# An order written out for the last unit of a quantized feed-forward, with accumulator banks in rotation, on one Trainium2 core

## The chip, the cores and the metric

One core of a Trainium2 chip. The metric is the device time of one execution in microseconds, the median of several runs. The engines named below are TensorE (PE in the profile; PEld is its weight load), VectorE (DVE), ScalarE (ACT), GpSimd (POOL) and SyncE (SP), which only starts transfers. Each engine has its own queue and works through it in order; an instruction that waits holds all that stands behind it on its engine.

## The reference

Two layers, each a conditioner (a linear map with a low-rank adapter chosen per batch) followed by a gated feed-forward, with a residual. The change lies in the second layer, whose feed-forward has weights of 4-bit integers with one scale for each 128 inputs:

```python
# x: (8, 128, 512), conditioner of layer 1
base_out = einsum('bti,oi->bto', x, W) + b
lora_out = einsum('btr,bro->bto', einsum('bti,bir->btr', x, A), Bm)
h = base_out + lora_out * 2.0
# feed-forward of layer 1: H = 512, I = 1792, groups of G = 128
W = q.reshape(O, In // G, G) * s[:, :, None]        # for gate, up and down
d = silu(einsum('bsh,ih->bsi', h, Wg)) * einsum('bsh,ih->bsi', h, Wu)
x = x + einsum('bsi,hi->bsh', d, Wd)
```

## The kernel before

All activations lie with features on partitions: `x[o]`, o = 0 to 3, holds 128 features of all 1024 tokens, and a "half" (tb = 0 or 1) is 512 tokens, the columns that one accumulator bank (PSUM) holds in float32. There are 8 banks.

**The conditioner of layer 1** makes h, four tiles of 128 features, as the sum of two parts, `hi` (rounded to the type float32r, in which these matmuls run) and `lo` (what the rounding left). Its products are made by a scheme with few multiplications, so results come out as sums of banks and helper tiles. The loop at lines 1300 to 1310 ends it: for m = 0 and 1, `l_added` (VectorE, line 1272) adds a bank to u[m], `l_finish` writes hi on ACT (line 1264) and then lo on VectorE (line 1266) for tile m, half 1; the same is then done with v[m] for tile m + 2, half 0. So h 3, half 0, is what comes last.

**The feed-forward** runs in 14 units f of 128 of the 1792 inner features. A unit has 8 products for gate (s = 0) and up (s = 1), one for each scale group k = 0 to 3, and, two units later (`LAG`), 4 products for down, one for each o. The integers are used as weights directly; the scale is applied when a bank is read. One product over 512 tokens is two matmuls, hi and lo (`summed`, line 1328). How each product leaves its banks:

- `scaled` without an addend runs on ACT (line 1334): it writes a fresh sum, or a copy `y` of a down product.
- `scaled` with an addend runs on VectorE (line 1337): bank times scale plus what is there, into `sum` or straight into `x[o]`.
- `added` runs on GpSimd (line 1343), for four things: the two partial gate sums are added (`gate_added`), the up sum is multiplied by the silu (`gated_q`), the lo part of the activation is made (`rest`, tile `act_lo`), and a copy y is added to x (`y_added`).
- ACT also makes the silu (line 1395) and the hi part of the activation (`first_bits`, line 1404, tile `act_hi`).

Thus a unit goes: gate sums, `gate_added` (GpSimd), silu (ACT), up sums, `gated_q` (GpSimd), `first_bits` (ACT), `rest` (GpSimd), and after that its down products may run. GpSimd also issues the loads of the integer weights (lines 1220 and 1222); the loads of units 10 to 13 wait until an earlier unit's buffer is free, and so are issued among the additions.

Units 0 to 12 run in the loop at line 1413, which sets the order on every engine. There a product covers both halves (two banks, a "pair", 4 matmuls, 1024 columns), with four pairs in rotation. The last unit, f = 13, and the down products of units 11, 12 and 13 run after it, by halves, in single banks taken from a pool of eight: first all eight products of half 0 with the down products of unit 11 between them, then half 1, then down of unit 12, then down of unit 13, each half of x[o] being stored when it has its last addend. Six halves of down products go through ACT, y and GpSimd there (o = 1 of units 11 and 12, half 0 of o = 3 of unit 12, half 0 of o = 1 of unit 13); the others are added by VectorE. The stores are at line 1515, on SP and ACT.

Of the kernel before, what the change touches and what calls it, by code (L numbers as in the profile page):

```python
# [7 lines left out]
F32 = mybir.dt.float32  # L8
# [3 lines left out]
ALU = mybir.AluOpType  # L12

P = 128
NB = 8
T = 1024
TB = 512
NTB = T // TB
# [16 lines left out]
WARM = 2  # L35
NS = H + NF * P
LAG = 2


@with_exitstack  # L40
def kernel(
# [1219 lines left out]
    def l_finish(o: int, tb: int, of):  # L1261
        hi, lo = (part[o][:, halves[tb]] for part in parts)
        plus = lb[:, o : o + 1]
        in_order(nc.scalar.activation(hi, of, AF.Identity, bias=plus))
        in_order(
            nc.vector.scalar_tensor_tensor(  # L1266
                lo, of, plus, hi.bitcast(F32), op0=ALU.add, op1=ALU.subtract
            )
        )

    def l_added(to, ps, plus):
        in_order(nc.vector.tensor_tensor(to, ps, plus, ALU.add))
# [27 lines left out]
    for m in two:  # L1300
        l_sum(3, m, "22", 5, False)
        l_sum(4, m, "T4", None, False)
        expand(
            [[None, banks[5, m]], [banks[4, m], None]], b1, [m * P, (m + 2) * P], [tl, tl],
            go_on={(0, 1)},
        )
        l_added(u[m], banks[5, m], u[m])
        l_finish(m, 1, u[m])
        l_added(v[m], banks[4, m], v[m])
        l_finish(m + 2, 0, v[m])  # L1310


# [6 lines left out]
    def pair(name: str):  # L1319
        return pairs.tile([P, NTB, TB], F32, tag="pair", name=name)  # L1320
# [4 lines left out]
    def summed(ps, w, src, at):  # L1325
        for n, part in enumerate(src):
            in_order(
                nc.tensor.matmul(ps, w, part[:, at], start=(n == 0), stop=(n == len(src) - 1))  # L1328
            )

    def scaled(to, ps, scale, plus=None):

        if plus is None:
            in_order(nc.scalar.activation(to, ps, AF.Identity, scale=scale))  # L1334
        else:
            in_order(
                nc.vector.scalar_tensor_tensor(  # L1337
                    to, ps, scale, plus, op0=ALU.mult, op1=ALU.add
                )
            )  # L1340

    def added(to, a, b, op):
        in_order(nc.gpsimd.tensor_tensor(to, a, b, op))  # L1343

    def unit_tile(what: str, f: int, bufs: int, dtype=F32):
        return l1.tile([P, T], dtype, tag=what, name=f"{what}_{f}", bufs=bufs)

    def gate_or_up(f: int, s: int, k: int, at=whole, into=None):


        on_act = k == 0 or (s == 0 and k == 2)
        if on_act and (f, s, k) not in sums:
            sums[f, s, k] = unit_tile(f"sum{s}{k}", f, 2)
        to = sums[f, s, k - k % 2 if s == 0 else 0][:, at]
        w, src = ready["q", f][0][:, s, k, :], [part[k] for part in parts]
        if into is None:
            both = pair(f"gu{s}_q{f}_{k}")
            for tb in range(NTB):
                summed(both[:, tb], w, src, halves[tb])
            ps = both.rearrange("p b s -> p (b s)")  # L1360
        else:
            summed(into, w, src, at)
            ps = into
        scaled(to, ps, sg[:, f, s, k : k + 1], None if on_act else to)

    def gate_added(f: int, at=whole):
        added(sums[f, 0, 0][:, at], sums[f, 0, 0][:, at], sums[f, 0, 2][:, at], ALU.add)

    def down_group(f: int, o: int, on_act=False, at=whole, into=None):
        w, src, scale = ready["q", f][1][:, bass.ts(o, P)], acts["q", f], sd[:, o, f : f + 1]  # L1370
        if into is None:
            both = pair(f"d_q{f}_{o}")
            for tb in range(NTB):
                summed(both[:, tb], w, src, halves[tb])
            ps = both.rearrange("p b s -> p (b s)")
        else:
            summed(into, w, src, at)
            ps = into
        to = x[o][:, at]
        if on_act:  # L1380
            if (f, o) not in ys:
                ys[f, o] = unit_tile("y", f"{f}_{o}", 2)
            scaled(ys[f, o][:, at], ps, scale)
        else:
            scaled(to, ps, scale, to)

    ys = {}

    def y_added(f: int, o: int, at=whole):
        added(x[o][:, at], x[o][:, at], ys[f, o][:, at], ALU.add)  # L1390

    def silu(f: int, at=whole):
        if ("sil", f) not in sums:
# [3 lines left out]
    def gated_q(f: int, at=whole):  # L1397
        if ("q", f) not in acts:
            acts["q", f] = [unit_tile(f"act_{w}", f, 3, F32R) for w in ("hi", "lo")]
        up = sums[f, 1, 0][:, at]  # L1400
        added(up, up, sums["sil", f][:, at], ALU.mult)

    def first_bits(f: int, at=whole):
        in_order(nc.scalar.copy(acts["q", f][0][:, at], sums[f, 1, 0][:, at]))  # L1404

    def rest(f: int, at=whole):
        hi, lo = acts["q", f]
        added(lo[:, at], sums[f, 1, 0][:, at], hi[:, at].bitcast(F32), ALU.subtract)
# [4 lines left out]
    for f in range(NF - 1):  # L1413
        d = f - LAG
        if d > 0 and d - 1 + QBUFS < NF:
            load_q(d - 1 + QBUFS)
        gate_or_up(f, 0, 0)
        if 0 < f <= LAG:
            silu(f - 1)
        gate_or_up(f, 0, 1 if f else 2)  # L1420
        if f:
            gated_q(f - 1)
        if d >= 0:
            down_group(d, 0)
        gate_or_up(f, 0, 2 if f else 1)
        if f:
            first_bits(f - 1)
            rest(f - 1)
        gate_or_up(f, 0, 3)
        gate_added(f)  # L1430
        if d >= 0:
            down_group(d, 1)
        for k in range(3):
            gate_or_up(f, 1, k)
        if d >= 0:
            down_group(d, 3, True)
            y_added(d, 3)
        if f >= LAG:
            silu(f)
        gate_or_up(f, 1, 3)  # L1440
        if d >= 0:
            down_group(d, 2)
# [2 lines left out]

    in_pairs.close()
    last = ctx.enter_context(
        tc.tile_pool(name="last", bufs=8, space=bass.MemoryType.PSUM, reuse_waits="tile")
    )

    def single(name: str):
        return last.tile([P, TB], F32, tag="bank", name=name)

    def down_half(f: int, o: int, tb: int, on_act: bool):
        down_group(f, o, on_act, halves[tb], single(f"d_q{f}_{o}_{tb}"))

    def down_halves(f: int, o: int, on_act: bool):
        for tb in range(NTB):
            down_half(f, o, tb, on_act)

    def y_halves_added(f: int, o: int):
        for at in halves:
            y_added(f, o, at)

    f = NF - 1

    def half_unit(s: int, k: int, tb: int):
        gate_or_up(f, s, k, halves[tb], single(f"gu{s}_q{f}_{tb}_{k}"))

    at = halves[0]  # L1470
    for s in range(2):
        for k in range(KC):
            half_unit(s, k, 0)
            if (s, k) == (0, 1):
                gated_q(f - 1)
            if (s, k) == (0, 2):
                first_bits(f - 1)
                rest(f - 1)
            if (s, k) == (0, 3):
                gate_added(f, at)  # L1480
            if k % 2 == 1:
                o = 2 * s + k // 2
                down_halves(f - LAG, o, o == 1)
                if o == 1:
                    y_halves_added(f - LAG, o)
            if (s, k) == (1, 0):
                silu(f, at)
    gated_q(f, at)

    d, at = f - 1, halves[1]
    for k in range(KC):
        half_unit(0, k, 1)
    gate_added(f, at)
    half_unit(1, 0, 1)
    silu(f, at)
    half_unit(1, 1, 1)
    first_bits(f, halves[0])
    rest(f, halves[0])  # L1500
    half_unit(1, 2, 1)
    half_unit(1, 3, 1)
    gated_q(f, at)
    down_halves(d, 1, True)
    down_halves(d, 0, False)
    first_bits(f, at)
    rest(f, at)
    y_halves_added(d, 1)
    down_half(d, 3, 0, True)
    y_added(d, 3, halves[0])  # L1510
    down_half(d, 3, 1, False)
    down_halves(d, 2, False)

    def store(engine, o: int, tb: int):
        in_order(engine.dma_start(out=out[:, o, halves[tb]], in_=x[o][:, halves[tb]]))

    for o in (1, 0, 2, 3):
        down_half(f, o, 0, o == 1)
        if o == 1:
            y_added(f, o, halves[0])  # L1520
        else:
            store(nc.sync, o, 0)
    for n, o in enumerate(range(KC)):
        down_half(f, o, 1, False)
        if n == 0:
            store(nc.scalar, 1, 0)
        store(nc.scalar if n % 2 else nc.sync, o, 1)


# [94 lines left out]
```

## Time and profile before

| | |
|---|---|
| time, median of 3 runs | 693.05 us (692.96 to 693.49) |
| the profiled execution | 693.4 us; span from first to last instruction 691.6 us |
| mean granted TensorE clock | 0.994 |
| busy, share of the span: PE, PEld | 674.3 us (97%), 381.7 us (55%) |
| busy: DVE, ACT, POOL | 446.0 us (64%), 185.8 us (27%), 365.4 us (53%) |
| feed-forward of layer 1, first matmul to last matmul's start | 518.19 to 684.31 us |
| its 14 x 48 = 672 matmuls, all in the trace, one each 0.227 us | 152.3 us |

The busy shares are averages over the whole kernel; this change touches the last 176 us only. There the times between the starts of neighbouring matmuls tell more than busy time, because the recorded duration of a matmul (0.39 us) overlaps the next.

### The profile page before, as it was taken

To read this page: it belongs to the slowest core of one execution; us is meant where nothing else is said; L and a number is where in the kernel's file an instruction comes from. 1 tells how busy PE (TensorE), PEld (TensorE's weight loads), DVE (VectorE), ACT (ScalarE), POOL (GpSimd) and SP (SyncE) were. 2 spreads that over 40 slices of the span, in tenths; PEclk is the share of its full clock that TensorE was granted. 3 is DMA by queue.
4 is the path that set the end of the run, shared out by engine and by line. 5 is a ranking of instruction groups with operands and counts; after the bars stand their busy time and mean duration, and the time that the engine had idled before them with its cause. 6 is when DMAs were issued, how large, how long until landed. Compare 5 with 4: busy or idle time off the path is not lost. (4 is left out here: it accounts for less than half of the span.)

```text
span 691.6 us, 6849 instructions
## 1 busy us (share of the span) xinstructions
PE 674.3 (97%) x2400; PEld 381.7 (55%) x2400; DVE 446.0 (64%) x636; ACT 185.8 (27%) x273; POOL 365.4 (53%) x324
## 2 busy tenths in 40 slices
PE   8999999999999999999999999999999999999994
PEld 3444444444444445666666654444436777788872
DVE  5545435435432578878787789253557888899985
ACT  1212112111100013333333320000025555566542
POOL 5257766240001064766966663044104889889885
PEclk9999999999999999999999999999999999999997
DMA  7501226030003002220200050006701211000003
GB/s 235 190 1 52 69 82 216 11 136 1 1 0 106 1 0 91 92 72 20 93 0 1 22 197 0 0 1 216 239 1 30 71 51 32 0 1 1 0 1 121
DMA packets 18333, 42.46 MB, mean 61 GB/s; under 512 B 3118, under 2 KB 4286, under 8 KB 18172
## 3 DMA queue, kind: packets, MB, share of 16 engines
q1 hardware_dynamic: 11628, 25.44, 10.7%
q0 software_dynamic: 5376, 14.49, 6.7%
q10 hardware_dynamic: 1296, 2.10, 0.9%
q8 instruction: 19, 0.31, 0.2%
q14 instruction: 14, 0.11, 0.1%
HBM read 39.93 MB, written 2.10 MB: 61 GB/s over the span
## 5 line engine op out<-in xcount | busy, mean ns | idle before, releaser
L1337 DVE SCALAR_TENSOR_TENSOR sum<-gu_q,sg,sum 128x1024 f32<-128x1024 f32 (+1 forms) x75 | 90.4, 1211 | 20.0 <-ACT sum L1334 14.8
L1328 PE MATMUL gu_q<-h_hi,wgu_q 128*128 128x512 f32 x224 | 88.8, 396 | 3.0 <-DVE x L1337 1.6
L1328 PE MATMUL gu_q<-h_lo,wgu_q 128*128 128x512 f32 x224 | 87.5, 391 | 0.3 <-DVE h_lo L1266 0.3
L1337 DVE SCALAR_TENSOR_TENSOR x<-d_q,sd,x 128x1024 f32<-128x1024 f32 (+1 forms) x51 | 54.3, 1087 | 4.0 <-POOL x L1343 4.0
L1343 POOL TENSOR_TENSOR sum<-sum,sum 128x1024 f32<-128x1024 f32 (+1 forms) x15 | 33.9, 2262 | 37.8 <-DVE sum L1337 37.8
L1334 ACT ACTIVATE sum<-gu_q,sg 128x1024 f32<-128x1024 f32 (+1 forms) x45 | 47.3, 1055 | 23.7 <-PE gu_q L1328 23.6
L73 PE MATMUL p_f<-x,s_f 128*128 128x512 f32 x112 | 52.2, 597 | 0.0
L1328 PEld LDWEIGHTS gu_q<-h_hi,wgu_q 128*128 128x128 f32 x224 | 42.0, 188 | 17.2 <-DVE x L1337 4.5
L1328 PE MATMUL d_q<-act_hi,wd_q 128*128 128x512 f32 x112 | 45.0, 401 | 3.8 <-ACT y L1334 3.3
L1328 PEld LDWEIGHTS gu_q<-h_lo,wgu_q 128*128 128x128 f32 x224 | 42.1, 188 | 8.9 <-DVE h_lo L1266 0.6
L1328 PE MATMUL d_q<-act_lo,wd_q 128*128 128x512 f32 x112 | 44.2, 395 | 0.3 <-POOL act_lo L1343 0.3
L73 PE MATMUL p_c<-x,raw_c 128*128 128x512 f32 x88 | 42.8, 607 | 1.0 <-DMA x<-in_xT_dram 0.5
L1343 POOL TENSOR_TENSOR act_lo<-sum,act_hi 128x1024 fp32r<-128x1024 f32 (+1 forms) x15 | 33.8, 2252 | 18.1 <-ACT act_hi L1404 16.8
L73 PE MATMUL p_c<-T_x,raw_c 128*128 128x512 f32 x88 | 41.6, 595 | 0.0
L574 DVE TENSOR_TENSOR act_c<-p_c,v_c 128x512 f32<-128x512 f32 x11 | 7.6, 691 | 52.2 <-PE p_c L73 52.2
L73 PE MATMUL p_c<-T_x,s_c 128*128 128x512 f32 x88 | 41.2, 592 | 0.0
L73 PE MATMUL p_f<-h,raw_f 128*128 128x512 f32 (+1 forms) x96 | 40.2, 541 | 0.1
L73 PE MATMUL d_f<-act_f,ds_f 128*128 128x512 f32 x84 | 36.6, 593 | 0.0
L73 PE MATMUL d_f<-act_f,wd_f 128*128 128x512 f32 x84 | 36.4, 592 | 0.0
L689 POOL TENSOR_TENSOR h<-h,dv_c 128x512 f32<-128x512 f32 x2 | 2.5, 1268 | 62.9 <-ACT dv_c L686 62.9
L1343 POOL TENSOR_TENSOR sum<-sum,sil_q 128x1024 f32<-128x1024 f32 (+1 forms) x15 | 33.9, 2261 | 2.8 <-ACT sil_q L1395 2.7
L575 POOL TENSOR_TENSOR act_c<-act_c,p_c 128x512 f32<-128x512 f32 x10 | 12.7, 1274 | 41.7 <-DVE act_c L574 33.0
(276 smaller groups left out, 1281.5 us busy)
## 6 DMA issues: line engine op xcount, KB each, us to landing
raw_f<-in_f_gu_dram SPq DMA_DIRECT2D x14, 512.0 KB
wgu_q<-in_q_gu_dram POOLq DMA_DIRECT2D x14, 512.0 KB
raw_c<-in_c_gu_dram SPq DMA_DIRECT2D x10, 512.0 KB
wd_f<-in_f_down_dram SPq DMA_DIRECT2D x14, 256.0 KB
wd_q<-in_q_down_dram POOLq DMA_DIRECT2D x14, 256.0 KB
x<-in_xT_dram SPq DMA_DIRECT2D x11, 256.0 KB
wd_c<-in_c_down_dram SPq DMA_DIRECT2D x11, 256.0 KB
x<-in_xT_dram ACTq DMA_DIRECT2D x5, 256.0 KB
```

The source lines that it names most:

```text
L73: in_order(nc_mm(*args, **kwargs))
L574: add(act[0], x4, v, ALU.add)
L575: mul(act[0], act[0], p1, ALU.mult)
L689: nc.gpsimd.tensor_tensor(at(m + 2, 1), at(m + 2, 1), v[m], ALU.add)
L1328: nc.tensor.matmul(ps, w, part[:, at], start=(n == 0), stop=(n == len(src) - 1))
L1334: in_order(nc.scalar.activation(to, ps, AF.Identity, scale=scale))
L1337: nc.vector.scalar_tensor_tensor(to, ps, scale, plus, op0=ALU.mult, op1=ALU.add)
L1343: in_order(nc.gpsimd.tensor_tensor(to, a, b, op))
```

## The change

Three edits.

1. In the conditioner's last loop the addition to v[m] moves ahead of the first `l_finish`.
2. In the loop over units: unit 0 runs its up group 0 before its gate group 3, and that gate group takes half 1 first (`turned`); `first_bits` and `rest` of unit 0 move from behind unit 1's gate group to behind its up group 2; the first down group of unit 0 (in unit 2) moves from behind gate group 1 to behind `gate_added`.
3. All that follows the loop is replaced by a list, `LAST`, that is worked through from left to right. Small letters are products or elementwise steps, capitals mostly the step that reads a product's bank: `g` and `G` for gate and up (digits: half, s, k), `d` and `D` for down with the sum in VectorE, `y` and `Y` for down through ACT and GpSimd (digits: units back from the last, o, half), `+`, `s`, `m`, `b`, `r` for gate_added, silu, gated_q, first_bits and rest of a half, `M`, `B`, `R` for the last three of unit 12. The n-th product takes bank n modulo 8. The list begins with half 1, mixes the two halves and the down products of units 11, 12 and 13, and sends six down products through y, all of them o = 1 except one half of o = 3. The gate sums of half 0 now go into one tile, so half 0 has no `gate_added`. A half of x[o] is stored when its third addend is in; from the fifth store on, every other one is issued by ACT.

The program of the changed kernel has the same 80 matmuls in this part, one more VectorE operation (29 of 512 columns), one GpSimd addition fewer, as many y copies (6), and 8 stores, of which SP issues 6 and ACT 2 (before: 5 and 3).

```diff
+LAST = """
+g100 g102 G102 g110 g103 G103 g111 G110 d231 G111 G100 g101 G101 g000 D231 M g001 g002 G000 d230
+g112 G001 d221 B +1 s1 g113 g010 d211 D230 G112 G002 G010 g011 G113 G011 g013 R g012 m1 y211
+D221 g003 b1 d201 Y211 G012 d131 d220 r1 G003 d120 G013 d210 d011 s0 D220 D131 d031 y210 m0 D201
+d101 b0 D120 Y210 D011 D031 d121 d130 y130 D121 d021 r0 Y130 d110 D021 d111 d001 d020 D101 y110
+y111 d010 y010 Y110 D001 D020 Y111 d100 D100 d030 d200 d000 D030 Y010 D200 D000
+"""
...
         l_added(u[m], banks[5, m], u[m])
+        l_added(v[m], banks[4, m], v[m])
         l_finish(m, 1, u[m])
-        l_added(v[m], banks[4, m], v[m])
         l_finish(m + 2, 0, v[m])
...
-    def gate_or_up(f: int, s: int, k: int, at=whole, into=None):
+    def gate_or_up(f: int, s: int, k: int, turned=False):
...
+        for tb in reversed(range(NTB)) if turned else range(NTB):
+            summed(both[:, tb], w, src, halves[tb])
...
         gate_or_up(f, 0, 1 if f else 2)
         if f:
             gated_q(f - 1)
-        if d >= 0:
+        if d > 0:
             down_group(d, 0)
         gate_or_up(f, 0, 2 if f else 1)
-        if f:
+        if f > 1:
             first_bits(f - 1)
             rest(f - 1)
-        gate_or_up(f, 0, 3)
+        if f == 0:
+            gate_or_up(f, 1, 0)
+        gate_or_up(f, 0, 3, f == 0)
         gate_added(f)
+        if d == 0:
+            down_group(d, 0)
         if d >= 0:
             down_group(d, 1)
-        for k in range(3):
+        for k in range(0 if f else 1, 3):
             gate_or_up(f, 1, k)
+        if f == 1:
+            first_bits(f - 1)
+            rest(f - 1)
...
     last = ctx.enter_context(
-        tc.tile_pool(name="last", bufs=8, space=bass.MemoryType.PSUM, reuse_waits="tile")
+        tc.tile_pool(name="last", bufs=1, space=bass.MemoryType.PSUM, reuse_waits="tile")
     )
...
+    turns = [last.tile([P, TB], F32, tag=f"bank{n}", name=f"bank{n}") for n in range(8)]
...
+    def next_bank(key, w, src, at):
+        n = len(groups)
+        ps = turns[n % 8]
+        groups[key] = ps
+        summed(ps, w, src, at)
...
+    def gate_up_out(tb: int, s: int, k: int):
+        apart = s == 0 and k >= 2 and tb == 1
+        to = sums[last_f, s, 2 if apart else 0][:, halves[tb]]
+        fresh = k == 0 or apart and k == 2
+        ps = groups["g", tb, s, k]
+        scaled(to, ps, sg[:, last_f, s, k : k + 1], None if fresh else to)
...
+    def store(o: int, tb: int):
+        waiting[o, tb] -= 1
+        if waiting[o, tb] == 0:
+            left.append((o, tb))
+            engine = nc.scalar if len(left) > 4 and len(left) % 2 else nc.sync
+            in_order(engine.dma_start(out=out[:, o, halves[tb]], in_=x[o][:, halves[tb]]))
...
+    def down_out(back: int, o: int, tb: int):
+        to = x[o][:, halves[tb]]
+        f = last_f - back
+        scaled(to, groups["d", back, o, tb], sd[:, o, f : f + 1], to)
+        store(o, tb)
...
+    def down_added(back: int, o: int, tb: int):
+        to = x[o][:, halves[tb]]
+        added(to, to, ys[back, o, tb], ALU.add)
+        store(o, tb)
...
+    for step in LAST.split():
+        steps[step[0]](*(int(c) for c in step[1:]))
```

More of the change, by code (lines that the diff above doesn't have):

```diff
@@ L1353, in gate_or_up @@
             sums[f, s, k] = unit_tile(f"sum{s}{k}", f, 2)
-        to = sums[f, s, k - k % 2 if s == 0 else 0][:, at]
+        to = sums[f, s, k - k % 2 if s == 0 else 0]
         w, src = ready["q", f][0][:, s, k, :], [part[k] for part in parts]
[L1356 to L1363, printed above, removed]
+        both = pair(f"gu{s}_q{f}_{k}")
+        for tb in reversed(range(NTB)) if turned else range(NTB):
+            summed(both[:, tb], w, src, halves[tb])
+        ps = both.rearrange("p b s -> p (b s)")
         scaled(to, ps, sg[:, f, s, k : k + 1], None if on_act else to)
@@ L1367, in gate_added, with down_group @@
         added(sums[f, 0, 0][:, at], sums[f, 0, 0][:, at], sums[f, 0, 2][:, at], ALU.add)
-    def down_group(f: int, o: int, on_act=False, at=whole, into=None):
+    def down_group(f: int, o: int, on_act=False):
         w, src, scale = ready["q", f][1][:, bass.ts(o, P)], acts["q", f], sd[:, o, f : f + 1]
[L1371 to L1379, printed above, removed]
+        both = pair(f"d_q{f}_{o}")
+        for tb in range(NTB):
+            summed(both[:, tb], w, src, halves[tb])
+        ps = both.rearrange("p b s -> p (b s)")
+        to = x[o]
         if on_act:
-            if (f, o) not in ys:
-                ys[f, o] = unit_tile("y", f"{f}_{o}", 2)
-            scaled(ys[f, o][:, at], ps, scale)
+            ys[f, o] = unit_tile("y", f"{f}_{o}", 2)
+            scaled(ys[f, o], ps, scale)
         else:
@@ L1387, with y_added @@
     ys = {}
-    def y_added(f: int, o: int, at=whole):
-        added(x[o][:, at], x[o][:, at], ys[f, o][:, at], ALU.add)
+    def y_added(f: int, o: int):
+        added(x[o], x[o], ys[f, o], ALU.add)
     def silu(f: int, at=whole):
@@ L1447 @@
     last = ctx.enter_context(
-        tc.tile_pool(name="last", bufs=8, space=bass.MemoryType.PSUM, reuse_waits="tile")
+        tc.tile_pool(name="last", bufs=1, space=bass.MemoryType.PSUM, reuse_waits="tile")
     )
[L1451 to L1470, printed above, removed]
-    for s in range(2):
[L1472 to L1520, printed above, removed]
-        else:
[L1522 to L1527, printed above, removed]
+    turns = [last.tile([P, TB], F32, tag=f"bank{n}", name=f"bank{n}") for n in range(8)]
@@ new lines, with gate_up_half @@
+    last_f = NF - 1
+    for s in range(2):
+        for k in (0, 2) if s == 0 else (0,):
+            sums[last_f, s, k] = unit_tile(f"sum{s}{k}", last_f, 2)
+    groups, left, y_halves = {}, [], []
+    waiting = {(o, tb): 3 for o in range(KC) for tb in range(NTB)}
+    def next_bank(key, w, src, at):
[3 more added lines that the diff above has]
+        summed(ps, w, src, at)
+    def gate_up_half(tb: int, s: int, k: int):
+        w = ready["q", last_f][0][:, s, k, :]
+        next_bank(("g", tb, s, k), w, [part[k] for part in parts], halves[tb])
@@ new lines, in gate_up_out, with down_half @@
+    def gate_up_out(tb: int, s: int, k: int):
[4 more added lines that the diff above has]
+        scaled(to, ps, sg[:, last_f, s, k : k + 1], None if fresh else to)
+    def down_half(back: int, o: int, tb: int):
+        f = last_f - back
+        next_bank(("d", back, o, tb), ready["q", f][1][:, bass.ts(o, P)], acts["q", f], halves[tb])
+    def store(o: int, tb: int):
[4 more added lines that the diff above has]
+            in_order(engine.dma_start(out=out[:, o, halves[tb]], in_=x[o][:, halves[tb]]))
@@ new lines, in down_out, with down_copied @@
+    def down_out(back: int, o: int, tb: int):
+        to = x[o][:, halves[tb]]
+        f = last_f - back
+        scaled(to, groups["d", back, o, tb], sd[:, o, f : f + 1], to)
+        store(o, tb)
+    def down_copied(back: int, o: int, tb: int):
+        n = len(y_halves)
+        if n % 2 == 0:
+            y_halves.append(unit_tile("y", f"last_{n}", 2))
+        else:
+            y_halves.append(y_halves[-1])
+        ys[back, o, tb] = y_halves[-1][:, halves[n % 2]]
+        f = last_f - back
+        scaled(ys[back, o, tb], groups["d", back, o, tb], sd[:, o, f : f + 1])
@@ new lines, in down_added @@
+    def down_added(back: int, o: int, tb: int):
+        to = x[o][:, halves[tb]]
+        added(to, to, ys[back, o, tb], ALU.add)
+        store(o, tb)
+    steps = {
+        "g": gate_up_half, "G": gate_up_out, "d": down_half, "D": down_out, "y": down_copied,
+        "Y": down_added, "+": lambda tb: gate_added(last_f, halves[tb]),
+        "s": lambda tb: silu(last_f, halves[tb]), "m": lambda tb: gated_q(last_f, halves[tb]),
+        "b": lambda tb: first_bits(last_f, halves[tb]), "r": lambda tb: rest(last_f, halves[tb]),
+        "M": lambda: gated_q(last_f - 1), "B": lambda: first_bits(last_f - 1),
+        "R": lambda: rest(last_f - 1),
+    }
```

## The prediction

> **What bounds the kernel now.** I read the waits of the last stage first, then each engine in order of time around its two ends, then busy time by stretch. Columns: start us, duration, engine, line, operation, tiles, shapes, count, [idle before it <-what ended it]. Where the stage begins, TensorE:
>
> ```profile
> 520.86 0.40 PE L1328 MATMUL gu_q<-h_lo,wgu_q 128*128 128x512 f32 x1
> 521.96 0.50 PE L1328 MATMUL gu_q<-h_hi,wgu_q 128*128 128x512 f32 x1 [0.70 <-ACT h_hi L1264]
> 522.74 0.50 PE L1328 MATMUL gu_q<-h_lo,wgu_q 128*128 128x512 f32 x1 [0.28 <-DVE h_lo L1266]
> ```
>
> A matmul starts every 0.227 us when nothing holds it (659.20 to 659.42); here 1.5 us are lost to h 3, made last. GpSimd after it:
>
> ```profile
> 525.50 2.41 POOL L1343 TENSOR_TENSOR sum<-sum,sum 128x1024 f32<-128x1024 f32 x1 [37.20 <-DVE sum L1337]
> 530.44 2.40 POOL L1343 TENSOR_TENSOR sum<-sum,sil_q 128x1024 f32<-128x1024 f32 x1 [2.04 <-ACT sil_q L1395]
> 534.01 2.38 POOL L1343 TENSOR_TENSOR act_lo<-sum,act_hi 128x1024 fp32r<-128x1024 f32 x1 [1.16 <-ACT act_hi L1404]
> ...
> 543.49 2.39 POOL L1343 TENSOR_TENSOR act_lo<-sum,act_hi 128x1024 fp32r<-128x1024 f32 x1 [1.16 <-ACT act_hi L1404]
> ...
> 555.33 2.40 POOL L1343 TENSOR_TENSOR act_lo<-sum,act_hi 128x1024 fp32r<-128x1024 f32 x1 [1.16 <-ACT act_hi L1404]
> ```
>
> From 543.49 on this is a closed loop, four additions at 2.36 us, one fixed idle of 1.16 us (ACT's act_hi), and the DMA issues of 0.58 us on the same queue: 11.84 us a unit, against 48 matmuls x 0.227 = 10.88 us. Its `act_lo` start at 555.33, 567.16, 578.43, 589.70; only without DMA issues (10.67 us, from 600.36) does TensorE set the pace. So until 600 us GpSimd does, and TensorE's pauses there (2.6 us after 549) follow it.
>
> Where the stage ends, TensorE and VectorE:
>
> ```profile
> 659.42 0.39 PE L1328 MATMUL gu_q<-h_lo,wgu_q 128*128 128x512 f32 x1
> 661.44 0.50 PE L1328 MATMUL gu_q<-h_hi,wgu_q 128*128 128x512 f32 x1 [1.63 <-DVE x L1337]
> ...
> 683.72 0.79 PE L1328 MATMUL d_q<-act_hi,wd_q 128*128 128x512 f32 x1 [1.76 <-ACT y L1334]
> ```
>
> ```profile
> 671.86 3.77 DVE L1337 SCALAR_TENSOR_TENSOR sum<-gu_q,sg,sum 128x512 f32<-128x512 f32 x5
> 675.55 4.69 DVE L1337 SCALAR_TENSOR_TENSOR x<-d_q,sd,x 128x512 f32<-128x512 f32 x7
> 684.20 3.38 DVE L1337 SCALAR_TENSOR_TENSOR x<-d_q,sd,x 128x512 f32<-128x512 f32 x5 [3.96 <-POOL x L1343]
> ```
>
> The last unit and the down parts beside it begin at 659.20. From there 80 matmuls (18.1 us) take until 684.94, because evacuations and GpSimd stand in their way; VectorE idles 3.96 us for a GpSimd addition and ends at 687.58. Then stores: 256 KB each at 385 GB/s (0.68 us), six of them crowded into 685.8 to 689.9.
>
> ```profile
> 676.00:680.00 4.00, 2.94 (x11) 1.91 (x11) 4.00 (x7) 2.18 (x4) 3.27 (x3) 1.00 0.00 0
> 680.00:684.00 4.00, 1.99 (x7) 1.15 (x7) 0.24 (x1) 0.69 (x1) 4.00 (x4) 0.97 0.35 131
> 684.00:688.00 4.00, 0.94 (x2) 0.22 (x2) 3.38 (x5) 0.00 (x0) 1.40 (x2) 0.50 0.56 207
> ```
>
> (Stretch, length, busy time of PE, PEld, DVE, ACT, POOL, then granted clock, DMA share, GB/s.)
>
> **The early part: u and v in a row, h 3 later, bits later.** No instruction is added; three orders change. (a) The second addition now stands ahead of the first finish on VectorE, so ACT can make h 3 as soon as it ends h 1: the h 3 pair of operations ends at 521.2 instead of 522.69. (b) Unit 0's up group 0 (four matmuls, 0.91 us) is put before the group that reads h 3, which also takes its finished half first: TensorE needs h 3 only at 522.5. The 1.5 us go, at no cost: up group 0 reads h 0, done by 515.9, and its two banks were released by the v addition at 519.7. (c) What GpSimd gets, by its own rows. Its first addition waits for VectorE's sum of gate group 3: that group ends on TensorE about 523.1, sum 1.27 us, so 524.55 (was 525.50). The silu behind it follows the first group of unit 1, which starts 1.4 us earlier: GpSimd's product at 529.05 (was 530.44). Now the split of unit 0 comes after the next gate addition (531.4, then 533.8 for act_lo, DMA issue 536.1), so GpSimd no longer waits 1.16 for act_hi nor 0.66 for the next silu; product of unit 1 at 536.7, and 3.56 us later (as 539.93 to 543.49) act_lo of unit 1 at 540.28: 3.2 us earlier. (d) ACT's sum of unit 1's up group 0, held behind act_hi until 533.83, passes; that held bank cost TensorE 0.7 us at 534.99. (e) The first down group moves to after the gate addition: it needs act_lo, ready 536.15, at 536.5. This cover is thin, 0.35 us; what act_lo loses beyond it, all matmuls behind it lose, but GpSimd's loop, which decides, does not.
>
> Since GpSimd sets the pace from there to 600 us, its shift is what all get: **-3.2 us**. Bounds: at least the 0.95 us of its first addition; at most 6.1 us, all TensorE pauses from 518 to 600 (1.5 + 2.4 + 2.2). I take the loop's own shift. So the last section starts at 656.0.
>
> **The last section.** Counts: 40 groups of two matmuls before and after, VectorE 28 to 29 operations of 512 columns, ACT copies 6 as before, GpSimd one gate addition of 512 less; the waits change. Times now from the section's start. TensorE: group n at 0.453n. Evacuation can start 0.76 after a group's start (661.44 to 662.30, less the 0.11 of a first matmul). VectorE is free of the old work at 2.15 (661.39 less the overlap). Its operations repeat every 0.66 (675.55 to 676.21) where neighbours write different halves, 0.85 (673.18 to 674.03) where an operation adds to what the one before wrote. Walking the list with ACT at 0.6, GpSimd at 2.36 and 1.26:
>
> - VectorE: 2.15 + 28 x 0.66 + 0.75 = 21.4; three neighbours add to the same half (x2 `D121 D021`, x0 `D101 D001`, `D200 D000`): 3 x 0.19. End **21.96**. No operation finds its group missing; the closest are G011 (ready 8.01, due 8.10), D220 (11.34, 11.40) and D100 (18.88, 19.04).
> - GpSimd: free at 2.15; M to 4.55, + to 5.8, R (its act_hi, 4.65 to 5.7, lies beside +) to 8.15, m1 at 8.3 (G113 done 8.2), Y211, r1 to 12.15, then m0, Y210, r0, Y130, Y110, Y111, Y010 without a gap: **20.9**, before VectorE.
> - TensorE: the handover from pairs costs nothing, since the pair evacuated last (2.19) is taken up by group 6 (2.72) and no longer by group 1: the 1.79 us go. Bank n comes back eight groups later; group 20 waits for D221 (0.5 us), 28 for D201 (0.2), 35 for D101 (about 1.0). Matmul r1's operand is due at 12.17, ready 12.15. The last group starts at 19.5. These waits cost nothing while VectorE has work: it ends 1.0 us after the last group could be evacuated.
> - Waits for whole engines: only d011 waits with many behind it (TensorE's 14 later groups for r1); VectorE then holds 1.9 us of earlier groups.
> - Stores: the last five are issued from 19.1 to 22.0 instead of six in 2.6 us, so the last finds the engines free: issue after 0.04, first packet 0.86 later (684.98 to 685.8), 0.68 for the packets, 1.70 to the end of the span: 3.28 (now 4.06). One store moves from ACT to SP: 0.33 us of issue, waited for by none but the next store.
>
> Sum: 656.0 + 21.96 + 3.28 = 681.2 against the profiled span of 691.64: -10.4 (-3.2 early, -6.4 section, -0.8 stores). That execution took 693.4, 0.35 above the median; 693.05 - 10.4 = **682.7 us**. Bounds of the section: no bubbles in VectorE, 21.4, gives 682.1; all of GpSimd's three act_hi idles of 1.16 kept gives 24.4 for its last addition and a store after it, so 685.2.
>
> The Trainium skill, VectorE: DVE Perf Modes, section "The DRAIN you can't avoid", says eight copies with a semaphore after each took as long as eight without, so waiting for the operation before would be free. By that rule the three bubbles vanish and the sum is 682.1; the rows (0.85 against 0.66) say otherwise.
>
> **Rivals.**
> 1. The loop takes the early gain back: only 0.95 us survive, as GpSimd meets a later wait (its gate addition waiting for VectorE, which carries a down group more in a row at unit 2). For it: the thin cover in (e). Against: loop idles are constant, 1.16. 682.7 + 2.25 = 685.0 us; 0.12.
> 2. The last section meets GpSimd idles: each handover to ACT and back costs 1.16 as in the loop. Against: every act_hi has another addition to lie beside. 685.2 us; 0.13.
> 3. Slower: cycling the banks makes TensorE pause so often that its clock drops to half through the last section. At 0.453 a matmul the section's matmuls take 36.3, evacuation and stores 1.3 + 3.3: span 696.9, 698.3 us. It is slower than now from a mean pitch of 0.39 us on (clock 0.58). Against: the pauses of 1.79 and 1.05 us left the clock at 1.00; 0.50 appears only after 684, with TensorE nearly done. 0.03. The Trainium skill, TensorE: Matmul & The Clock Gate, section "A second HAM failure mode: psum-queue depth-cycling", tells of a kernel that cycled PSUM so and whose clock oscillated; here eight banks already rotate, at 1.00.
> 4. The list doesn't take effect: ruled out nearly, each engine's program has the listed order. 693; 0.01.
>
> **How the numbers follow.** Forecast 0.71 (own range 681.4 to 684.2). Runs tell 0.2% (1.4 us) from no change. Faster: forecast, rivals 1 and 2, 0.96; same 0.01; slower 0.03. The range reaches down to 681.0 (bubbles gone and the store tail shorter by a queue's worth) and up to 686.2, past rivals 1 and 2, both with a microsecond of their kind more: 0.85 inside.
>
> **What would show it.** TensorE without a pause at 521 to 523 and at the section's start; act_lo of unit 1 about 540.3; section start near 656; VectorE solid from 658 to 678, GpSimd ending 1 us before it; clock 1.00 to the end of the matmuls. Wrong if GpSimd's loop starts no earlier than 542.5, if VectorE idles over 1 us in the section, or if TensorE waits for act_lo in d011.

## The result and the profile after

| | before | after |
|---|---|---|
| time, median (lowest to highest), 4 runs each on one chip | 693.12 us (692.96 to 693.49) | 683.96 us (683.85 to 684.07) |
| profiled execution: time, span | 693.4, 691.64 us | 684.07, 682.35 us |
| last section, from its first matmul to VectorE's end | 659.20 to 687.58 | 655.78 to 677.69 |
| VectorE's end to the end of the span | 4.06 us | 4.66 us |

The ratio is 0.9867 (95% interval 0.985 to 0.9884). The forecast of 682.7 us was 1.3 us too low.

First GpSimd in order of time, where the stage begins and in units 0 to 2 (start us, duration, engine, line, operation, tiles, shapes, count, [idle before it <-what ended it]):

```profile
524.52 2.40 POOL L1358 TENSOR_TENSOR sum<-sum,sum 128x1024 f32<-128x1024 f32 x1 [35.90 <-DVE sum L1352]
...
528.86 2.41 POOL L1358 TENSOR_TENSOR sum<-sum,sil_q 128x1024 f32<-128x1024 f32 x1 [1.42 <-ACT sil_q L1401]
531.24 2.39 POOL L1358 TENSOR_TENSOR sum<-sum,sum 128x1024 f32<-128x1024 f32 x1
533.60 2.41 POOL L1358 TENSOR_TENSOR act_lo<-sum,act_hi 128x1024 fp32r<-128x1024 f32 x1
...
540.15 2.40 POOL L1358 TENSOR_TENSOR act_lo<-sum,act_hi 128x1024 fp32r<-128x1024 f32 x1 [1.16 <-ACT act_hi L1410]
...
551.97 2.41 POOL L1358 TENSOR_TENSOR act_lo<-sum,act_hi 128x1024 fp32r<-128x1024 f32 x1 [1.16 <-ACT act_hi L1410]
```

The act_lo of unit 0 has no idle time in front of it any more: the next gate addition fills the time in which ACT makes act_hi. The act_lo of unit 1 starts 3.34 us earlier than before, that of unit 2 3.36 (551.97 against 555.33), the last section 3.42 (655.78 against 659.20).

TensorE has no pause around 521 to 523 and none when the pairs are handed over to single banks at 655.78: the second product (656.24) follows the first without a gap, where before it started 2.02 us behind the matmul before it (659.42 to 661.44). In the last section two of its pauses show a releaser; for VectorE the view shows no idle time in the same stretch:

```profile
655.78 0.39 PE L1343 MATMUL bank<-h_hi,wgu_q 128*128 128x512 f32 x1
656.01 0.39 PE L1343 MATMUL bank<-h_lo,wgu_q 128*128 128x512 f32 x1
656.24 0.39 PE L1343 MATMUL bank<-h_hi,wgu_q 128*128 128x512 f32 x1
...
665.30 0.50 PE L1343 MATMUL bank<-act_hi,wd_q 128*128 128x512 f32 x1 [0.27 <-DVE x L1352]
...
673.40 0.50 PE L1343 MATMUL bank<-act_hi,wd_q 128*128 128x512 f32 x1 [0.67 <-DVE x L1352]
```

```profile
656.70 1.27 DVE L1352 SCALAR_TENSOR_TENSOR x<-d_q,sd,x 128x1024 f32<-128x1024 f32 x1
657.90 2.08 DVE L1352 SCALAR_TENSOR_TENSOR sum<-bank,sg,sum 128x512 f32<-128x512 f32 x3
...
665.16 2.06 DVE L1352 SCALAR_TENSOR_TENSOR sum<-bank,sg,sum 128x512 f32<-128x512 f32 x3
667.14 10.55 DVE L1352 SCALAR_TENSOR_TENSOR x<-bank,sd,x 128x512 f32<-128x512 f32 x15
```

Where before VectorE idled 3.96 us for GpSimd, the last 15 operations now run in one piece and end at 677.69. The last additions of GpSimd end a microsecond earlier:

```profile
671.58 5.03 POOL L1358 TENSOR_TENSOR x<-x,y_last 128x512 f32<-128x512 f32 x4
```

By stretch (length, busy PE, PEld, DVE, ACT, POOL, granted clock, DMA share, GB/s) both of these engines are full to the end, and the clock is 1.00 as long as TensorE works:

```profile
668.00:672.00 4.00, 4.00 (x18) 3.07 (x18) 3.90 (x7) 2.50 (x5) 4.00 (x4) 1.00 0.00 0
672.00:676.00 4.00, 3.29 (x14) 2.06 (x12) 3.90 (x6) 1.36 (x3) 4.00 (x4) 1.00 0.59 220
676.00:680.00 4.00, 0.00 (x0) 0.00 (x0) 1.58 (x3) 0.00 (x0) 0.61 (x1) 0.91 0.81 305
680.00:682.30 2.30, 0.00 (x0) 0.00 (x0) 0.00 (x0) 0.00 (x0) 0.00 (x0) 0.50 0.00 0
```

The last row is the surprise. For 2.3 us no engine computes and nothing is transferred, yet the span goes on. The page does not count the instructions that stand there; the raw records of the trace do. Start us, duration, engine, operation:

```
before  683.71  6.362  GpSimd  DRAIN
        690.57  0.007  Sync    DRAIN
        690.60  0.017  GpSimd  EVENT_SEMAPHORE
after   674.97  6.308  GpSimd  DRAIN
        677.71  0.333  Sync    DMA_DIRECT2D     (the last store)
        679.75  0.028  Sync    EVENT_SEMAPHORE  (its wait for that store is over)
        679.87  0.007  Sync    DRAIN
        681.32  0.017  GpSimd  EVENT_SEMAPHORE
        682.29  0.017  Sync    EVENT_SEMAPHORE
```

At the program's end each engine drains and reports, and GpSimd's semaphore instruction goes on only when all have. GpSimd's own drain (its record starts while the last additions still run) ends long after the last of them: 681.28 less 676.61 is 4.67 us; before, 690.07 less 685.40, again 4.67. Before, that lay hidden behind the last store (SyncE was done at 690.57). Now the store is back at 679.75, SyncE is done at 679.87, and everybody waits for GpSimd until 681.3.

### The profile page after: what moved, and what is told of

The parts are those of the page before. It is cut to its first block, busy times and chain, and to the rows that moved or that the text cites. A ratio compares the mean times of both kernels' runs of the same rounds, so it can differ in the third digit from the quotient of the medians.

```text
span 682.3 us, 6850 instructions
## 1 busy us (share of the span) xinstructions
PE 672.0 (98%) x2400; PEld 382.9 (56%) x2400; DVE 446.3 (65%) x637; ACT 185.4 (27%) x272; POOL 369.9 (54%) x323
## 4 chain that ended last, share of the span: by engine, by line
PE 87%; POOL 7%; issue 3%; DMA 1%; DVE 1%; ACT 1%; ACTq 0%; POOLq 0%; DVEq 0%
PE p_c L88 21%; PE p_f L88 14%; PE d_f L88 12%; PE d_c L88 11%; PE gu_q L1343 10%; PE d_q L1343 5%; PE l L88 4%; PE zb_f L88 3%; PE za_f L88 3%; POOL sum L1358 2%; POOL act_lo L1358 1%; PE bank L1343 1%; POOL x L1358 1%; DMA x<-in_xT_dram 1%; POOL s L308 1%
## 5 line engine op out<-in xcount | busy, mean ns | idle before, releaser
L1352 DVE SCALAR_TENSOR_TENSOR sum<-gu_q,sg,sum 128x1024 f32<-128x1024 f32 x65 | 83.1, 1283 | 14.8 <-ACT sum L1349 10.9
L1343 PE MATMUL gu_q<-h_hi,wgu_q 128*128 128x512 f32 x208 | 82.0, 394 | 0.2 <-ACT sum L1349 0.2
L1343 PE MATMUL gu_q<-h_lo,wgu_q 128*128 128x512 f32 x208 | 81.2, 390 | 0.0
L1349 ACT ACTIVATE sum<-gu_q,sg 128x1024 f32<-128x1024 f32 x39 | 43.1, 1112 | 21.1 <-PE gu_q L1343 21.0
L1343 PEld LDWEIGHTS gu_q<-h_hi,wgu_q 128*128 128x128 f32 x208 | 39.0, 188 | 12.0 <-DVE x L1352 2.4
L1343 PEld LDWEIGHTS gu_q<-h_lo,wgu_q 128*128 128x128 f32 x208 | 39.1, 188 | 7.9
L1352 DVE SCALAR_TENSOR_TENSOR x<-d_q,sd,x 128x1024 f32<-128x1024 f32 x33 | 42.0, 1275 | 0.0
L1343 PE MATMUL d_q<-act_hi,wd_q 128*128 128x512 f32 x88 | 34.7, 394 | 0.2 <-DVE sum L1352 0.2
L1343 PE MATMUL d_q<-act_lo,wd_q 128*128 128x512 f32 x88 | 34.3, 390 | 0.0
```

The costliest lines, as they stand in the source:

```text
L1352: nc.vector.scalar_tensor_tensor(to, ps, scale, plus, op0=ALU.mult, op1=ALU.add)
```

## The experiments

All times are medians beside runs of the kernel before on the same chip (693.1 to 693.2 us). "After" is the changed kernel. One trace is one execution, and these differ: in the eight kernels that are the same up to there, GpSimd's first addition starts anywhere from 524.30 to 524.92 us. Where tenths matter, times are therefore counted from the start of the stretch in question.

### The two ends by themselves

`early_only`: edits 1 and 2 alone, the code behind the loop as before.

```diff
         l_added(u[m], banks[5, m], u[m])
-        l_finish(m, 1, u[m])
         l_added(v[m], banks[4, m], v[m])
+        l_finish(m, 1, u[m])
...
-        gate_or_up(f, 0, 3)
+        if f == 0:
+            gate_or_up(f, 1, 0)
+        gate_or_up(f, 0, 3, turned=f == 0)
...
+        if d == 0:
+            down_group(d, 0)
...
+        if f == 1:
+            first_bits(f - 1)
+            rest(f - 1)
...
```

> The kernel before with edits 1 and 2 alone (conditioner's last loop and loop over units), its own last section kept. Theory: GpSimd's loop starts 3.2 us earlier and nothing takes it back, so the old last section starts at 656.0 instead of 659.2: 693.1 - 3.2 = 689.9 us. Rival (the gain is taken back on the way): 692 to 693 us.

Measured 689.86 us (689.55 to 690.7), ratio 0.9957 [0.9943, 0.9972]: 3.2 us from the early part.

`last_only`: edit 3 alone, conditioner and loop as before.

```diff
-        l_added(v[m], banks[4, m], v[m])
         l_finish(m, 1, u[m])
+        l_added(v[m], banks[4, m], v[m])
...
-        if d > 0:
+        if d >= 0:
             down_group(d, 0)
...
-        if f > 1:
+        if f:
             first_bits(f - 1)
             rest(f - 1)
...
```

> The changed kernel with edits 1 and 2 undone, only the listed last section kept. Theory: the parts add up, the section starts at 659.2 and takes what it takes in the changed kernel (26.3 us to the span's end): 684.0 + 3.2 = 687.2 us. Rival (the listed section needs the earlier start of GpSimd to fit): 688 us or more.

Measured 687.51 us (687.5 to 688.12), ratio 0.9919 [0.9903, 0.9936]: 5.6 us. The two parts make 8.8 of the 9.2 us; they touch different ends and add up to within the scatter.

`no_uv`: after with edit 1 undone (h 3 late again, the loop's new order kept).

```diff
-        l_added(v[m], banks[4, m], v[m])
         l_finish(m, 1, u[m])
+        l_added(v[m], banks[4, m], v[m])
```

> The changed kernel with edit 1 alone undone (first finish again ahead of the addition to v). Theory: ACT's h 3 comes at 521.18 and ACT's first sum behind it at 521.81 instead of 520.27, so the first pair of banks is free at 522.9 where the fifth pair wants it at 522.0: all behind is 0.9 us later, 684.9 us. Rival A (the moved groups of edit 2 hide it all): 684.0. Rival B (all of the first pauses come back): 685.5.

Measured 685.13 us (684.81 to 685.23), ratio 0.9883 [0.9867, 0.99], 1.2 us above after. GpSimd's first addition starts at 525.47 instead of 524.52, its act_lo of unit 1 at 541.22 instead of 540.15 (1.07 later). The wait is the one that was expected: TensorE pauses from 521.86 to 522.80 for a bank that ACT's sum releases. So with the loop's new order in place, one line of the conditioner is worth 1.2 of the early 3.2 us; what it would be worth alone was not run.

### What sets the end

`pool_more`: one more addition on GpSimd (into a tile nobody reads afterwards, so the output is the same) behind its last one; no store depends on it. If the stores set the end, it costs nothing.

```diff
-... D030 Y010 D200 D000
+... D030 Y010 z D200 D000
...
+        "z": lambda: added(*[sums["sil", last_f][:, halves[1]]] * 3, ALU.add),
```

> The changed kernel with one more GpSimd addition of 512 columns, on a tile nobody reads again, behind GpSimd's last addition: the output is the same. Theory: the end waits for GpSimd, whose last instruction ends 4.67 us after its last addition (676.61 to 681.28), while the last store has landed at 679.75; so one addition of 1.25 us more costs 1.25: 685.2 us. Rival (the last store, or VectorE before it, sets the end): 684.0 us, no change.

Measured 685.03 us (684.78 to 685.47), ratio 0.9882 [0.9866, 0.9899]: 1.1 us more. The records (columns as above):

```
pool_more  675.31  7.240  GpSimd  DRAIN
           680.19  0.007  Sync    DRAIN
           682.60  0.017  GpSimd  EVENT_SEMAPHORE
```

The added instruction ran from 676.85 to 677.89 (1.04 us, not the 1.25 expected), the drain ended 4.67 later at 682.55, the barrier came right behind it, while SyncE had been done since 680.2. This is the test that settles the tail: GpSimd's last instruction sets the end although no data wait for it.

`d010`: the reverse, one addition taken off GpSimd's end; the last of its half products is added by VectorE.

```diff
-y111 d010 y010 Y110 D001 D020 Y111 d100 D100 d030 d200 d000 D030 Y010 D200 D000
+y111 d010 Y110 D001 D020 Y111 d100 D100 d030 d200 d000 D030 D200 D010 D000
```

> The changed kernel with the last down product that goes through ACT and GpSimd (o = 1, half 0, last unit) added by VectorE instead, between D200 and D000. VectorE: one operation more (0.66), one pair of neighbours on the same half less (0.19): ends 0.47 later; GpSimd ends 1.25 earlier. If the end waits for GpSimd: the bound passes to the last store, SP done at 680.3 instead of GpSimd at 681.3, so 683.0 us. If the last store sets the end: 684.4 us.

Measured 682.99 us (682.48 to 683.03), ratio 0.9851 [0.9834, 0.9867], 1.0 us below after, though VectorE, full already, got an operation more.

```
d010  672.55  7.332  GpSimd  DRAIN
      680.10  0.028  Sync    EVENT_SEMAPHORE
      680.23  0.007  Sync    DRAIN
      680.26  0.017  GpSimd  EVENT_SEMAPHORE
```

GpSimd's drain ends at 679.88 (4.67 after its last addition at 675.2), now before the last store, and the barrier is SyncE's again.

`apart`: the list reordered so that no two neighbours of VectorE add to the same half, but for the last pair.

```diff
-D201 d101 b0 D120 Y210 D011 D031 d121 d130 y130 D121 d021 r0 Y130 d110 D021 d111 d001 d020 D101 y110
+D201 d101 b0 D120 Y210 D011 d121 d130 y130 D121 D031 d021 r0 Y130 d110 d111 d001 d020 D101 D021 y110
```

> The changed kernel with D121 moved ahead of D031 and D101 ahead of D021 in the list, so that two of the three neighbours on VectorE that add to the same half stand apart. Both theories: VectorE ends 0.38 us earlier (2 x 0.19). If the end waits for GpSimd: time unchanged, 684.0 us. If the last store sets it: 683.6 us.

Measured 683.75 us (683.36 to 683.88), ratio 0.9862 [0.9846, 0.9879]. It is 0.2 below after and 0.15 above the rival's 683.6, so the time decides nothing; the trace does. VectorE's last 15 operations:

```profile
666.98 10.15 DVE L1352 SCALAR_TENSOR_TENSOR x<-bank,sd,x 128x512 f32<-128x512 f32 x15
```

They take 10.15 us instead of 10.55, and only the last pair still starts 0.84 apart. VectorE ends 21.51 us after the section's start instead of 21.91, and SyncE is done at 679.48. GpSimd's last addition ends where it did (20.82 against 20.83), its drain at 681.11, and the barrier follows at 681.15. VectorE's and SyncE's earlier end leaves the end of the kernel where GpSimd puts it.

### The banks

`pool_banks`: the same list, but the banks come from a rotating pool of eight in the order in which the pool hands them out, as before, instead of n modulo 8.

```diff
-        tc.tile_pool(name="last", bufs=1, space=bass.MemoryType.PSUM, reuse_waits="tile")
+        tc.tile_pool(name="last", bufs=8, space=bass.MemoryType.PSUM, reuse_waits="tile")
...
-    turns = [last.tile([P, TB], F32, tag=f"bank{n}", name=f"bank{n}") for n in range(8)]
...
-        ps = turns[n % 8]
+        ps = last.tile([P, TB], F32, tag="bank", name=f"bank_{n}")
```

> The changed kernel with the list's products taking banks from a pool of eight in the pool's own order, as the last section before the change did, not by number modulo 8; the order on every engine stays. In its program the second product then waits for the pair that is evacuated last. Theory: TensorE pauses 1.8 us there as in the kernel before, VectorE gets its first sums late and idles about as long: 685.7 us. Rival (VectorE has other work meanwhile, the rotation itself is worth nothing): 684.0 us.

Measured 685.73 us (685.53 to 685.98), ratio 0.9891 [0.9875, 0.9908]: 1.8 us more. TensorE and VectorE at the start of the section:

```profile
655.89 0.39 PE L1343 MATMUL bank<-h_lo,wgu_q 128*128 128x512 f32 x1
657.90 0.50 PE L1343 MATMUL bank<-h_hi,wgu_q 128*128 128x512 f32 x1 [1.62 <-DVE x L1352]
```

```profile
659.70 2.08 DVE L1352 SCALAR_TENSOR_TENSOR sum<-bank,sg,sum 128x512 f32<-128x512 f32 x3 [1.85 <-PE bank L1343]
```

The second product gets a bank that VectorE is still to read, and the handover pause of the kernel before is back (655.89 to 657.90 instead of one matmul's 0.227: 1.78 us). VectorE starts 1.8 later and cannot make it up, and GpSimd, which sets the end, ends 22.76 us after the section's start instead of 20.83. So of the last section's 5.6 us, 1.8 hang on the order in which the banks come.

### The loop

`d03`: in unit 2 the down product o = 3 of unit 0 (the third in the loop's order) is added by VectorE instead of through ACT and GpSimd: one GpSimd addition fewer just where GpSimd was thought to set the pace.

```diff
-            down_group(d, 3, True)
-            y_added(d, 3)
+            down_group(d, 3, d > 0)
+            if d > 0:
+                y_added(d, 3)
```

> The changed kernel with the third down group of unit 0 added by VectorE, not through ACT and GpSimd: one GpSimd addition of 1024 columns (2.36 us) less in the loop, one VectorE operation of 1.2 us more. Theory (GpSimd's loop paces the stage from 540 to 600 us): all behind comes 1.9 us earlier, as far as VectorE's later up sums let GpSimd go on, and TensorE's pauses after 546 (2.6 us) shrink by as much: 682.1 us. Rival (TensorE or VectorE paces it): 684.0 us or some tenths more.

Measured 683.97 us (683.91 to 684.63), ratio 0.987 [0.9854, 0.9887]: nothing. GpSimd, then ACT:

```profile
539.92 2.40 POOL L1358 TENSOR_TENSOR act_lo<-sum,act_hi 128x1024 fp32r<-128x1024 f32 x1 [1.17 <-ACT act_hi L1410]
...
551.12 2.42 POOL L1358 TENSOR_TENSOR act_lo<-sum,act_hi 128x1024 fp32r<-128x1024 f32 x1 [2.58 <-ACT act_hi L1410]
```

```profile
548.99 1.12 ACT L1349 ACTIVATE sum<-gu_q,sg 128x1024 f32<-128x1024 f32 x1 [2.21 <-PE gu_q L1343]
550.00 1.03 ACT L1410 CAST act_hi<-sum 128x1024 fp32r<-128x1024 f32 x1
```

From one act_lo to the next it is 11.20 us instead of 11.82: of an addition of 2.36 only 0.6 arrive. The idle time before act_lo grew from 1.16 to 2.58, because the act_hi it waits for stands on ACT behind a sum that waits 2.21 us for TensorE, and TensorE itself paused there, from 545.66 to 546.83, for banks that ACT still held. The section then starts 0.6 earlier, counted from GpSimd's first addition, but takes VectorE 0.56 longer (22.47 against 21.91 us). At its start TensorE paused 0.25 at 656.02 and 0.27 at 657.21; for these two the trace shows no releaser.

`cyc`: the loop's four pairs also taken strictly in turn, as a test whether bank order is at work in the loop too.

```diff
-        tc.tile_pool(name="pairs", bufs=4, space=bass.MemoryType.PSUM, reuse_waits="tile")
+        tc.tile_pool(name="pairs", bufs=1, space=bass.MemoryType.PSUM, reuse_waits="tile")
...
+    four = [pairs.tile([P, NTB, TB], F32, tag=f"pair{n}", name=f"pair{n}") for n in range(4)]
...
-        return pairs.tile([P, NTB, TB], F32, tag="pair", name=name)
+        return four[(len(taken) - 1) % 4]
```

> The changed kernel with the four pairs of banks of the loop over units taken strictly in turn, not in the pool's own order; a control for the next two. No pause of TensorE before 600 us is put down to the pool's order, so no change: 683.7 to 684.3 us. Rival (the pool's order causes part of the 2.5 us of pauses between 544 and 600): 681.5 to 683.5 us.

Measured 684.48 us (684.21 to 684.61), ratio 0.9874 [0.9858, 0.9891]; 0.5 more than after. TensorE now waits 0.52 us before 519.25 for the v addition, which still reads a bank that it needs; but it had started 0.49 earlier (517.70 against 518.19), and its fifth matmul comes when it did (519.25 against 519.22). In the trace the section starts 0.16 later than in after, so it does not show where the 0.5 comes from. Turns are no gain in themselves.

`y0_cyc`: `cyc`, and the copy y of unit 0 is added to x by VectorE instead of GpSimd (ACT's part stays).

```diff
     def y_added(f: int, o: int):
-        added(x[o], x[o], ys[f, o], ALU.add)
+        if f == 0:
+            in_order(nc.vector.tensor_tensor(x[o], x[o], ys[f, o], ALU.add))
+        else:
+            added(x[o], x[o], ys[f, o], ALU.add)
```

> The control (pairs in turn) with the addition of y of unit 0 to x moved from GpSimd to VectorE; order and bank waits of TensorE are the same. Theory (GpSimd's loop paces the stage from 540 to 600 us): GpSimd's lo part of unit 2 starts 1.2 us earlier, as far as ACT's hi part behind TensorE's third gate group allows, and all behind follows: the control less 1.2. Rival (TensorE or VectorE paces it): the control's time, or up to a microsecond more for VectorE's extra 1.2 us.

Measured 684.72 us (684.26 to 685.04), ratio 0.9877 [0.986, 0.9893]: again no gain. GpSimd, then VectorE:

```profile
543.08 2.42 POOL L1361 TENSOR_TENSOR sum<-sum,sum 128x1024 f32<-128x1024 f32 x1
...
547.92 2.40 POOL L1361 TENSOR_TENSOR sum<-sum,sil_q 128x1024 f32<-128x1024 f32 x1 [1.36 <-DVE sum L1355]
...
552.40 2.40 POOL L1361 TENSOR_TENSOR act_lo<-sum,act_hi 128x1024 fp32r<-128x1024 f32 x1 [2.08 <-ACT act_hi L1416]
```

```profile
544.32 2.25 DVE L1400 TENSOR_TENSOR x<-x,y 128x1024 f32<-128x1024 f32 x1
```

The moved addition held VectorE for 2.25 us, GpSimd's product behind it waited 1.36 for VectorE's sum, and act_lo came 11.70 after the one before (540.70) instead of 11.82. Here too its act_hi stood on ACT behind a sum that waited for TensorE (2.68 us).

### Together

`all3` joins `apart`, `d010` and `d03`; `best_cyc` joins `y0_cyc`, `apart` and `d010`. Their edits are those above.

> The last three edits together: neighbours apart, o = 1 half 0 of the last unit by VectorE, third down group of unit 0 by VectorE. If the end waits for GpSimd and the loop paces the stage, the parts add up: -1.9 from the loop; VectorE ends +0.66 - 0.57 = 0.1 later within the section, and the end is the last store's, 1.4 earlier than GpSimd's now: 680.7 us. Rival (neither): 684.1 us.

> The last kernel with the two edits of the end as well (neighbours on the same half apart; o = 1, half 0 of the last unit added by VectorE). Theory: the gains add up, 1.2 in the loop and 1.2 at the end: the control less 2.4, about 681.6 us. Rival (no gain in the loop): 682.8 us.

`all3` measured 682.82 us (682.44 to 683.25), ratio 0.9849 [0.9833, 0.9866], the fastest kernel of the study and about as fast as `d010` alone. `best_cyc` measured 683.55 us (682.64 to 683.76), ratio 0.9857 [0.984, 0.9873]. Both lack what their loop edits were to bring; in `all3` GpSimd's idle before act_lo of unit 2 is 2.57 us, as in `d03`. At the end the two paths now meet: GpSimd's drain ends at 680.41 and 680.75, SyncE's at 680.35 and 680.68, so by these two traces taking more off either one alone would gain less than 0.1 us.

## Why the prediction was right, and where it was short

**The early part** came as worked out, step by step: first addition 524.52 (forecast 524.55), product 528.86 (529.05), gate addition 531.24 (531.4), act_lo of unit 0 533.60 (533.8), of unit 1 540.15 (540.28), section start 655.78 (656.0). `early_only` gives it 3.2 us, the number of the sum, and `no_uv` shows that it moves with GpSimd's first steps. Rival 1, the loop taking it back, did not come.

**That GpSimd alone sets the pace until 600 us** was the reason given, and it is only half shown. A later start shifts everything by as much (`no_uv`), and the intervals equal GpSimd's own work plus 1.16. But taking work off GpSimd in unit 2 brought its act_lo forward by 0.6 and about 0.1 us in place of the 1.9 and 1.2 forecast: a chain from ACT's sums through TensorE's banks lies close behind, and in these runs it took over (in `y0_cyc` VectorE's longer queue adds to it). TensorE's pauses after the change fit this without proving it: after 519, 0.2 us before 544 and 2.55 from there to 600. What a kernel with both chains shortened would gain was not tried.

**The last section**: VectorE ends 21.91 us after the start (forecast 21.96), GpSimd 20.83 (20.9). The last 15 operations are 14 x 0.66 + 0.75 = 9.99 and take 10.55: the difference is three times 0.19, the three bubbles counted from the rows. They are real: in `apart` two go and 0.40 us with them, in `all3`, with no such neighbours left, the 15 take 9.96. While GpSimd sets the end they cost no time that these runs can show. TensorE's predicted waits of 0.5, 0.2 and about 1.0 measured 0.54, 0.19 and 0.93, and d011 did not wait for act_lo. No handover pause; `pool_banks` prices it at 1.8 us, as the 1.79 of the forecast. Rival 2, idles of GpSimd, did not come.

**The clock**, rival 3: 1.00 in every stretch to 676, with eight banks in strict turn and pauses up to 0.83 us. What the Trainium skill, TensorE: Matmul & The Clock Gate, section "A second HAM failure mode: psum-queue depth-cycling", tells of another kernel, a clock that swings to and fro, did not show here.

**The step that failed is the last term of the sum, the stores: 3.28 us forecast, 4.66 measured.** Its "1.70 to the end of the span" was carried over from the trace of before, where the store was the last thing the barrier waited for. The stores themselves did what was forecast: SyncE was done at 679.87, and in `d010`, where SyncE was the last, the span of 681.3 ends 1.04 us after the barrier's instruction at 680.26. By that the stores alone would give a tail of 679.87 + 0.03 + 1.04 - 677.69 = 3.25. But the prediction passed over GpSimd's 20.9 as "before VectorE", with only its data in mind. GpSimd's end, 676.61, plus 4.67 us of drain is 681.28, and 682.3 with the last microsecond. `pool_more` and `d010` show this from both sides. With it the forecast would have been 656.0 + 20.9 + 4.67 + 1.0 = 682.6 for the span, and 1.4 more (693.05 less 691.64) for the median: 684.0. Of the 1.4 us that the stores' term was short, the section's start, 0.22 earlier than forecast, hides a part.

## What to carry to other kernels

The end of a kernel has one path for each engine, not only that of the stores: add to each engine's last instruction what the trace of before shows behind it, even where that lay hidden, and take work off the engine with the longest one first. A pause where accumulators pass from one use to the next can hang on which buffer the pool hands out first, so look at the order and not only at the count. Regular intervals that equal one engine's work do not prove that it alone sets the pace; take one instruction away and see what arrives.

## What the runs showed of the hardware

- GpSimd's drain at the program's end finishes 4.67 us after its last addition in all fourteen traces, though the drain's own record is between 6.3 and 7.4 us long; VectorE's ends within 0.1 us of its last operation (677.74 against 677.69 in after).
- VectorE's addition of two tiles in SBUF, 128x1024, took 2.25 us in `y0_cyc`, started while a GpSimd addition ran from 543.08 to 545.50. From that end it is 1.08 us to its own. The Trainium skill, SBUF — State Buffer, section "Who interferes with whom", says that VectorE with two inputs in SBUF contends with a GpSimd instruction that reads SBUF, and that the order of issue decides who blocks. Two executions agree, both with GpSimd's addition started first: in `best_cyc` it took 2.25 us again, and again 1.08 of them behind the end of the GpSimd addition. This instruction was not run without GpSimd beside it; the nearest is the lo part of h, 512 columns from two tiles in SBUF, which took 0.75 us in before while GpSimd was idle (521.94). VectorE's operations with one input in a bank are not held up in after: from 668 to 672 they follow each other at their usual pace while GpSimd is busy for all of the 4.00 us.
- A pool of eight buffers did not hand them out in the order that n modulo 8 gives: with nothing else changed its order cost 1.8 us (`pool_banks`).
